# Turning adjacency masks by transposing DMA transfers in a two-layer graph-attention kernel

## The chip, the cores and the metric

The kernel runs on one core of one Trainium2 chip. The metric is the device time of one execution in microseconds (us). A core has several engines that work side by side, each through its own queue in order: TensorE (PE; its weight loads are shown apart as PEld), VectorE (DVE), ScalarE (ACT), GpSimd (POOL) and SyncE (SP), which issues most loads. Sixteen DMA engines move data between HBM and SBUF for all of them. Matrix products land in PSUM[...].

## The reference

Two graph-attention layers over 2708 nodes with 1024 features, each behind a layer norm and with a residual. What matters here is that both layers mask their scores with the adjacency matrix:

```python
# layer 0, x is relu(layernorm(input))
f = x @ Wf + bf
g = x @ Wg + bg
e = jax.nn.relu(f @ g.T)
scores = jnp.where(adj > 0, e, NEG)            # adj: 2708 x 2708 int32
attention = jax.nn.softmax(scores, axis=1)
return attention @ (x @ W + bW)
# layer 1: e = leaky_relu(f1 + f2.T), the same mask, softmax, attention @ h, relu
```

## The kernel before

The nodes are cut into five panels of columns: two of width 586 and three of width 512. A panel is computed with the scores transposed: the 128 partitions of a tile hold the nodes attended to, and its columns the nodes of the panel. The nodes on the partitions come in 11 pairs of tiles, mostly two times 128 rows; one pair has two times 74. Products of blocks use Strassen's scheme in Winograd's form, with seven products (M1 to M7) in place of eight, in fp32.

As the adjacency lies in memory by row, its block must be transposed for this layout. A maker of masks per panel has three steps: `fetch` loads int32 blocks; `convert` makes 0 or -2^100 of them in bf16 on VectorE; `turn` transposes.

```python
    WX, HX = wide, wide // 2                       # wide = 586
    ...
    def mask_maker(p):
        r0, w = panels[p][0][0], width[p]
        k4 = w // P                                # 4; P = 128
        tail = w - k4 * P                          # 74 or 0
        ...
        def convert(q):
            n = rows_of[q]
            a, b = raw.pop(q)
            m = [slot("nm", (P, k4, 2, P), BF)]
            nc.vector.tensor_scalar(m[0][:, :, :, :n], a[:, :, :, :n], 0.0, -BIG, op0=OP.is_le, op1=OP.mult)
            ...
        def turn(q):
            n = rows_of[q]
            m = neg.pop(q)
            mk = slot("mask", (P, 2, WX), BF)
            ps = bank("mk_ps", (P, 2, W), BF)
            for k in range(2):
                for i in range(k4):
                    nc.tensor.transpose(ps[:n, k, i * P:(i + 1) * P], m[0][:, i, k, :n], identb)
            nc.scalar.copy(mk[:n, :, :k4 * P], ps[:n, :, :k4 * P])
            if tail:
                ...                                # the same for the last 74 columns, in another bank
            nc.gpsimd.dma_start(mk_d[p][:n, q], mk[:n, :, :w])   # kept in HBM for layer 1
            mk_sb[p, q] = mk
```

The scores of a panel use it one pair ahead (`behind` puts pieces of other work between the products):

```python
        for q in range(NQ):                        # 11 pairs
            make_until(q + 2)                      # panel 0: norms and transposed rows, hs_d
            if q + 2 < NQ:
                fetch(q + 2)
            ...
            product(q, M1, X, True)                # each loads its operands As from hs_d
            if left_over:
                left_over()                        # M4 of the pair before, finish(q - 1, sb, 1)
            product(q, M6, Z, True)
            product(q, M5, Y, True)
            add(t[:n, hi], Y[:n, :h], m1[:n, hi])
            if q + 1 < NQ:
                convert(q + 1)
            behind(rate, True)
            product(q, M2, X, False)
            ...
            product(q, M7, Z, False)
            ...
            product(q, M3, Y, False)
            add(sa[:n, hi], Y[:n, :h], t[:n, lo])
            finish(q, sa, 0)                       # max(s, 0) + mask on VectorE, running maximum
            if q + 1 < NQ:
                turn(q + 1)
            behind(2 * rate, True)
```

The masks of each panel's first pair are made ahead of its scores by `first_masks`. Layer 1 loads the masks from `mk_d` and does not turn them again. The instructions' order in the queues is chosen by a scheduler from the program's order and its dependences, except where VectorE's order is held.

Of the kernel before, what the change touches and what calls it, by code (L numbers as in the profile page):

```python
# [9 lines left out]
BF = mybir.dt.bfloat16  # L10
I32 = mybir.dt.int32
AF = mybir.ActivationFunctionType
OP = mybir.AluOpType
AX = mybir.AxisListType

BIG = 2.0 ** 100
EPS = 1e-5
ALPHA = 0.2
P = 128
W = 512  # L20
# [36 lines left out]
def kernel(  # L57
# [19 lines left out]
    nc = InOrder(tc)  # L77
# [5 lines left out]
    wide = (N - 3 * W) // 2  # L83
# [6 lines left out]
    tiles = [t for q in panels for t in q]  # L90
# [4 lines left out]
    pairs = []  # L95
# [5 lines left out]
    NQ = len(pairs)  # L101
    pair_of = {t: (q, k) for q, ts in enumerate(pairs) for k, t in enumerate(ts)}
    rows_of = [tiles[a][1] for a, _ in pairs]
    WX, HX = wide, wide // 2

    consts = ctx.enter_context(tc.tile_pool(name="consts", bufs=1))
    slots = ctx.enter_context(tc.tile_pool(name="slots", bufs=54))
# [6 lines left out]
    def slot(name, shape=(P, WX), dt=FP):  # L114
        return slots.tile(list(shape), dt, tag="slot", name=name)

    def stream(name, shape=(P, D), dt=FP):
        return strm.tile(list(shape), dt, tag="strm", name=name)

    def load(o, i):  # L120
        tc.keep_in_program_order(nc.sync.dma_start(o, i))

    def bank(name, shape=(P, W), dt=FP):
        return psum.tile(list(shape), dt, tag="bank", name=name)
# [15 lines left out]

    ident = consts.tile([P, P], FP, name="ident")
    make_identity(nc, ident)
    identb = consts.tile([P, P], BF, name="identb")
    nc.vector.tensor_copy(identb, ident)
    eps = consts.tile([P, 1], FP, name="eps")
    nc.vector.memset(eps, EPS)
    ones = consts.tile([P, 1], FP, name="ones")
# [16 lines left out]
    def one():  # L164
        for it in later[:2]:
            if it[1]:
                it[1]()
                it[1] = None
        us, _, go = later.pop(0)[:3]
        go()  # L170
        return us

    def behind(us, psum_free=False):
        credit[0] = min(credit[0] + us, 2 * us)
        while later and credit[0] > 0 and (psum_free or not later[0][3]) and (not later[0][4] or later[0][4]()):
            credit[0] -= one()
# [41 lines left out]
    def add(o, a, b):  # L218
        nc.vector.tensor_tensor(o, a, b, OP.add)
# [354 lines left out]
    def mask_maker(p):  # L574

        r0, w = panels[p][0][0], width[p]
        k4 = w // P
        tail = w - k4 * P
        raw, neg = {}, {}

        def fetch(q):
            a = stream("adj_i", (P, k4, 2, P), I32)
            b = slot("adj_t", (P, 2, P), I32) if tail else None
            raw[q] = a, b
            (j0, n), (j1, _) = (tiles[t] for t in pairs[q])
            body = adj[r0:r0 + k4 * P].rearrange("(i p) j -> p i j", p=P)
            last = adj[r0 + k4 * P:r0 + w]
            if j1 == j0 + P:
                load(a.rearrange("p i k j -> p i (k j)"), body[:, :, j0:j0 + 2 * P])
                if tail:  # L590
                    load(b[:tail].rearrange("p k j -> p (k j)"), last[:, j0:j0 + 2 * P])
            else:
                for k, j in enumerate((j0, j1)):
                    load(a[:, :, k, :n], body[:, :, j:j + n])
                    if tail:
                        load(b[:tail, k, :n], last[:, j:j + n])

        def convert(q):
            n = rows_of[q]
            a, b = raw.pop(q)  # L600
            m = [slot("nm", (P, k4, 2, P), BF)]
            nc.vector.tensor_scalar(m[0][:, :, :, :n], a[:, :, :, :n], 0.0, -BIG, op0=OP.is_le, op1=OP.mult)
            if tail:
                m.append(slot("nmt", (P, 2, P), BF))
                nc.vector.tensor_scalar(m[1][:tail, :, :n], b[:tail, :, :n], 0.0, -BIG, op0=OP.is_le, op1=OP.mult)
            neg[q] = m

        def turn(q):
            n = rows_of[q]
            m = neg.pop(q)  # L610
            mk = slot("mask", (P, 2, WX), BF)
            ps = bank("mk_ps", (P, 2, W), BF)
            for k in range(2):
                for i in range(k4):
                    nc.tensor.transpose(ps[:n, k, i * P:(i + 1) * P], m[0][:, i, k, :n], identb)  # L615
            nc.scalar.copy(mk[:n, :, :k4 * P], ps[:n, :, :k4 * P])  # L616
            if tail:
                ps = bank("mk_ps", (P, 2, W), BF)
                for k in range(2):
                    nc.tensor.transpose(ps[:n, k, :tail], m[1][:tail, k, :n], identb[:tail, :tail])  # L620
                nc.scalar.copy(mk[:n, :, k4 * P:w], ps[:n, :, :tail])
            nc.gpsimd.dma_start(mk_d[p][:n, q], mk[:n, :, :w])
            mk_sb[p, q] = mk

        return fetch, convert, turn
# [272 lines left out]
    def scores(p, B):  # L898

        w = width[p]  # L900
        h = w // 2
        lo, hi = slice(0, h), slice(h, w)
        fetch, convert, turn = makers[p]
        rb = slot("rb")
        spread(rb, [r_[:n, first[p] + i:first[p] + i + 1] for i, (_, n) in enumerate(panels[p])])
        acc = slot("acc")
        S = [None] * NT
        rate = (0.6, 1.0, 0.65, 0.65, 0.65)[p]
        lefts = {}

        def product(q, m, ps, start):
            n, i = rows_of[q], BY_SCORES.index(m)
            if i % 2 == 0:
                t = stream("As", (P, 2, NH, P))
                lefts[q] = t
                k = min(2, 7 - i)
                if n == P:
                    load(t[:, :k].rearrange("p m c j -> p (m c j)"),
                         hs_d[q][:, i:i + k].rearrange("p m c j -> p (m c j)"))
                else:  # L920
                    load(t[:, :k, :, :n].rearrange("p m c j -> p (m c) j"),
                         hs_d[q][:, i:i + k, :, :n].rearrange("p m c j -> p (m c) j"))
            for c in range(NH):
                nc.tensor.matmul(ps[:n, :h], lefts[q][:, i % 2, c, :n], B[m][c // 2][:, c % 2, :h],  # L924
                                 start=(start and c == 0), stop=(c == NH - 1), skip_group_check=True)

        def finish(q, s, k):

            n, mk = rows_of[q], mk_sb[p, q]
            nc.vector.scalar_tensor_tensor(s[:n, :w], s[:n, :w], 0.0, mk[:n, k, :w], op0=OP.max, op1=OP.add)  # L930
            if q == 0 and k == 0:
                nc.vector.tensor_copy(acc[:, :w], s[:, :w])
            else:
                nc.vector.tensor_tensor(acc[:n, :w], acc[:n, :w], s[:n, :w], OP.max)
            if q in known:
                raise_max(p, q, k, mk[:n, k, :w])

        def last(q, sb, Z, m1):

            n = rows_of[q]  # L940
            product(q, M4, Z, False)
            add(sb[:n, lo], Z[:n, :h], m1[:n, lo])
            finish(q, sb, 1)
            mk_sb.pop((p, q))
            behind(rate, True)

        nc.hold = True
        left_over = None
        for q in range(NQ):
            n = rows_of[q]  # L950
            make_until(q + 2)
            if q + 2 < NQ:
                fetch(q + 2)
            sa, sb = slot("Sa"), slot("Sb")
            S[pairs[q][0]], S[pairs[q][1]] = sa, sb
            X, Y, Z = (bank(f"s{k}") for k in "xyz")
            m1, t = slot("sm1"), slot("st")
            product(q, M1, X, True)
            for s in (lo, hi):
                add(m1[:n, s], X[:n, :h], rb[:n, s])  # L960
            if left_over:
                left_over()
            product(q, M6, Z, True)
            add(t[:n, lo], Z[:n, :h], m1[:n, hi])
            behind(rate, True)
            product(q, M5, Y, True)
            add(t[:n, hi], Y[:n, :h], m1[:n, hi])
            if q + 1 < NQ:
                convert(q + 1)
            behind(rate, True)  # L970
            product(q, M2, X, False)
            add(sa[:n, lo], X[:n, :h], rb[:n, lo])
            behind(rate, True)
            product(q, M7, Z, False)
            add(sb[:n, hi], Z[:n, :h], t[:n, hi])
            behind(rate, True)
            product(q, M3, Y, False)
            add(sa[:n, hi], Y[:n, :h], t[:n, lo])
            finish(q, sa, 0)
            if q + 1 < NQ:  # L980
                turn(q + 1)
            behind(2 * rate, True)
            left_over = lambda q=q, sb=sb, Z=Z, m1=m1: last(q, sb, Z, m1)
        left_over()
        nc.hold = False
        return S, acc
# [279 lines left out]
```

## Time and profile before

| What | Before |
|---|---|
| time, median of 3 | 3197.63 us (3196.51 to 3199.61) |
| span of the profiled execution | 3194.6 us |
| mean granted TensorE clock | 0.992 |
| DMA in the whole span | 649.93 MB, mean 203 GB/s |
| transposes of masks, full blocks | 440, and 44 of the tails |
| copies of masks out of PSUM | 55 of the full blocks, 22 of the tails |
| masks stored to HBM | 55 transfers |

How to read it: the span is the time of one profiled execution. A line of the costliest groups gives line of the program, engine, operation, output and inputs, then count, busy time, mean duration in ns, and the engine's idle time just before with what ended most of it. A duration of a matmul or transpose on TensorE overlaps with its neighbours'. A line of waits gives who waited for whom: us in total, times, longest. A DMA queue's line gives packets, MB, and the time of its packets as a share of 16 engines over the stretch. The helper line L44 stands for all VectorE operations.

### The profile page before, as it was taken

How to read it: one execution, taken by the hardware profiler on the slowest of the kernel's cores; microseconds unless marked ns; L12 is line 12 of the kernel's file. 1: busy time of each engine (PE TensorE's matmuls, PEld its weight loads, DVE VectorE, ACT ScalarE, POOL GpSimd, SP SyncE). 2: the span in 40 equal slices, each digit the busy share in tenths (PEclk: the TensorE clock that was granted, in tenths of full speed). 3: DMA queues.
4: the chain of work that ended last, by engine and by line, in shares of the span. 5: the costliest groups of instructions: out<-in, count | busy, mean ns of one | idle time of the engine just before them, and what ended most of it. 6: DMA issues, size and time to landing. Idle time of an engine off the chain costs nothing.

```text
span 3194.6 us, 35414 instructions
## 1 busy us (share of the span) xinstructions
PE 3124.2 (98%) x12934; PEld 2327.1 (73%) x12934; DVE 1757.6 (55%) x3606; ACT 507.7 (16%) x853; POOL 380.3 (12%) x476
## 2 busy tenths in 40 slices
PE   8999999999999999999999999998999999999998
PEld 5576776667877588876888886865757748778685
DVE  7957676375722686427671358658474371643712
ACT  4412120010200112001020002103031130211200
POOL 3623102110002110011000101020010000000001
PEclk9999999999999999999999999999999999999999
DMA  6958848776446586477755567695655455565655
GB/s 258 330 189 284 284 131 318 216 235 198 165 128 182 173 272 198 147 210 228 246 163 155 163 205 235 200 305 195 206 169 164 142 171 170 186 187 176 195 155 205
DMA packets 284334, 649.93 MB, mean 203 GB/s; under 512 B 51254, under 2 KB 116746, under 8 KB 284160
## 3 DMA queue, kind: packets, MB, share of 16 engines
q1 hardware_dynamic: 243744, 522.94, 51.8%
q0 software_dynamic: 40416, 124.72, 11.5%
q8 instruction: 103, 1.69, 0.2%
q14 instruction: 71, 0.58, 0.1%
HBM read 533.96 MB, written 113.58 MB: 203 GB/s over the span
## 4 chain that ended last, share of the span: by engine, by line
PE 83%; issue 8%; DVE 4%; POOL 2%; DMA 2%; ACT 1%; SPq 0%; POOLq 0%; DVEq 0%; ACTq 0%
PE gz L478 13%; PE gy L478 13%; PE gx L478 12%; PE sz L924 8%; PE sy L924 5%; PE sx L924 5%; PE pz L822 5%; PE gv L478 4%; PE M_ps L413 3%; PE qz L478 3%; PE py L822 3%; PE px L822 3%; PE qy L478 2%; PE qx L478 2%; PE mk_ps L615 1%
## 5 line engine op out<-in xcount | busy, mean ns | idle before, releaser
L924 PE MATMUL sz<-B,As 128*128 128x256 f32 (+3 forms) x1320 | 323.1, 393 | 0.7 <-DVE st L44 0.7
L924 PEld LDWEIGHTS sz<-B,As 128*128 128x128 f32 (+1 forms) x1320 | 245.1, 186 | 58.3 <-DVE st L44 1.7
L924 PE MATMUL sx<-B,As 128*128 128x256 f32 (+3 forms) x880 | 225.0, 399 | 10.2 <-DMA As<-hs_d 9.2
L756 POOL TENSOR_TENSOR gT<-gT,rr 128x2048 f32<-128x2048 f32 (+3 forms) x20 | 68.3, 3432 | 1274.6 <-DVE rr L44 475.7
L924 PE MATMUL sy<-B,As 128*128 128x256 f32 (+3 forms) x880 | 218.8, 391 | 0.0
L478 PE MATMUL gz<-Sa,hc 128*128 128x256 f32 (+3 forms) x880 | 206.6, 393 | 0.0
L478 PE MATMUL gz<-P,hc 128*128 128x256 f32 (+3 forms) x880 | 206.3, 393 | 0.0
L478 PE MATMUL gx<-P,hc 128*128 128x256 f32 (+3 forms) x880 | 202.6, 392 | 0.1
L478 PE MATMUL gy<-T,hc 128*128 128x256 f32 (+3 forms) x880 | 202.5, 391 | 0.0
L924 PEld LDWEIGHTS sx<-B,As 128*128 128x128 f32 (+1 forms) x880 | 161.3, 188 | 46.3 <-issue 11.4
L478 PEld LDWEIGHTS gx<-P,hc 128*128 128x128 f32 (+1 forms) x880 | 167.1, 190 | 35.7 <-issue 2.0
L478 PEld LDWEIGHTS gy<-T,hc 128*128 128x128 f32 (+1 forms) x880 | 166.9, 190 | 34.0
L924 PEld LDWEIGHTS sy<-B,As 128*128 128x128 f32 (+1 forms) x880 | 162.8, 185 | 37.7 <-DVE st L44 0.3
L478 PEld LDWEIGHTS gz<-Sa,hc 128*128 128x128 f32 (+1 forms) x880 | 165.5, 190 | 31.9
L478 PEld LDWEIGHTS gz<-P,hc 128*128 128x128 f32 (+1 forms) x880 | 165.5, 190 | 31.9
L822 PE MATMUL px<-w,gT 128*128 128x512 f32 x320 | 145.5, 607 | 12.5 <-issue 11.1
L822 PE MATMUL py<-w,ps 128*128 128x512 f32 (+1 forms) x352 | 155.3, 592 | 0.0
L822 PE MATMUL pz<-w,ps 128*128 128x512 f32 (+1 forms) x352 | 155.1, 592 | 0.0
L616 ACT COPY mask<-mk_ps 128x1024 bf16<-128x1024 bf16 (+1 forms) x55 | 55.6, 1011 | 555.5 <-PE mk_ps L615 274.2
L822 PEld LDWEIGHTS pz<-w,ps 128*128 128x128 f32 (+1 forms) x352 | 65.4, 186 | 85.6 <-issue 82.0
L822 PEld LDWEIGHTS py<-w,ps 128*128 128x128 f32 (+1 forms) x352 | 65.4, 186 | 85.1 <-issue 82.9
L822 PEld LDWEIGHTS px<-w,gT 128*128 128x128 f32 x320 | 61.6, 195 | 88.7 <-issue 84.1
(261 smaller groups left out, 4790.6 us busy)
## 6 DMA issues: line engine op xcount, KB each, us to landing
hc<-hg_d SPq DMA_DIRECT2D x350, 512.0 KB
As<-hs_d SPq DMA_DIRECT2D x150, 512.0 KB
w<-wt_d SPq DMA_DIRECT2D x96, 512.0 KB
w<-in_L_gnn_W_dram SPq DMA_DIRECT2D x72, 512.0 KB
md<-md_d SPq DMA_DIRECT2D x56, 512.0 KB
adj_i<-in_adj_dram SPq DMA_DIRECT2D x50, 512.0 KB
hg_d<-g POOLq DMA_DIRECT2D x40, 512.0 KB, 5.0
hs_d<-hsT POOLq DMA_DIRECT2D x40, 512.0 KB, 6.1
```

What stands on the lines that cost most here:

```text
L413: nc.tensor.matmul(ps, wfT[a][c // NH][:, c % NH, :], wgT[b][c], start=(c == 0), stop=(c == NC - 1))
L478: nc.tensor.matmul(ps[d], left(m, k, d), right(m, k), start=(start and k == 0), stop=(k == K - 1), skip_group_check=True)
L615: nc.tensor.transpose(ps[:n, k, i * P:(i + 1) * P], m[0][:, i, k, :n], identb)
L616: nc.scalar.copy(mk[:n, :, :k4 * P], ps[:n, :, :k4 * P])
L756: nc.gpsimd.tensor_tensor(of(e, s), of(e, s), by(s, k), OP.mult)
L822: nc.tensor.matmul(ps, left[i][m][:, k, :], w_[k], start=(start and k == 0), stop=(k == NH - 1), skip_group_check=True)
L924: nc.tensor.matmul(ps[:n, :h], lefts[q][:, i % 2, c, :n], B[m][c // 2][:, c % 2, :h], start=(start and c == 0), stop=(c == NH - 1), skip_g ...
```

## The change

`turn` no longer uses TensorE, PSUM and ScalarE's copies. Each block of 128 x 256 bf16 (the two halves of a pair side by side) is transposed by one DMA transfer from SBUF to SBUF, issued from ScalarE's queue; a tail is padded from 74 to 80 rows and takes one more. For this the mask's row is padded from 586 to 592 columns, the padding of the tail's source is cleared on VectorE, short pairs load and convert full blocks of 128 columns, and the identity in bf16 is dropped. `turn` is called straight after `convert`, as its transfers have a latency. It is meant to take the transposes out of TensorE's queue.

```diff
-    WX, HX = wide, wide // 2
+    HX = wide // 2
+    WX = -(-wide // 16) * 16
...
-    identb = consts.tile([P, P], BF, name="identb")
-    nc.vector.tensor_copy(identb, ident)
...
+        tail16 = -(-tail // 16) * 16
...
-                    load(a[:, :, k, :n], body[:, :, j:j + n])
+                    load(a[:, :, k, :], body[:, :, j:j + P])
...
-            nc.vector.tensor_scalar(m[0][:, :, :, :n], a[:, :, :, :n], 0.0, -BIG, op0=OP.is_le, op1=OP.mult)
+            nc.vector.tensor_scalar(m[0], a, 0.0, -BIG, op0=OP.is_le, op1=OP.mult)
             if tail:
                 m.append(slot("nmt", (P, 2, P), BF))
-                nc.vector.tensor_scalar(m[1][:tail, :, :n], b[:tail, :, :n], 0.0, -BIG, op0=OP.is_le, op1=OP.mult)
+                nc.vector.memset(m[1][tail // 32 * 32:tail16], 0.0)
+                nc.vector.tensor_scalar(m[1][:tail], b[:tail], 0.0, -BIG, op0=OP.is_le, op1=OP.mult)
...
             mk = slot("mask", (P, 2, WX), BF)
-            ps = bank("mk_ps", (P, 2, W), BF)
-            for k in range(2):
-                for i in range(k4):
-                    nc.tensor.transpose(ps[:n, k, i * P:(i + 1) * P], m[0][:, i, k, :n], identb)
-            nc.scalar.copy(mk[:n, :, :k4 * P], ps[:n, :, :k4 * P])
+            for i in range(k4):
+                nc.scalar.dma_start_transpose(mk[:, :, i * P:(i + 1) * P], m[0][:, i].rearrange("p k j -> p (k j)"))
             if tail:
-                ps = bank("mk_ps", (P, 2, W), BF)
-                for k in range(2):
-                    nc.tensor.transpose(ps[:n, k, :tail], m[1][:tail, k, :n], identb[:tail, :tail])
-                nc.scalar.copy(mk[:n, :, k4 * P:w], ps[:n, :, :tail])
+                nc.scalar.dma_start_transpose(mk[:, :, k4 * P:k4 * P + tail16],
+                                              m[1][:tail16].rearrange("p k j -> p (k j)"))
...
             if q + 1 < NQ:
                 convert(q + 1)
+                turn(q + 1)
...
             finish(q, sa, 0)
-            if q + 1 < NQ:
-                turn(q + 1)
             behind(2 * rate, True)
```

More of the change, by code (lines that the diff above doesn't have):

```diff
@@ L584, in fetch @@
             raw[q] = a, b
-            (j0, n), (j1, _) = (tiles[t] for t in pairs[q])
+            j0, j1 = (tiles[t][0] for t in pairs[q])
             body = adj[r0:r0 + k4 * P].rearrange("(i p) j -> p i j", p=P)
@@ L593, in fetch @@
                 for k, j in enumerate((j0, j1)):
-                    load(a[:, :, k, :n], body[:, :, j:j + n])
+                    load(a[:, :, k, :], body[:, :, j:j + P])
                     if tail:
-                        load(b[:tail, k, :n], last[:, j:j + n])
+                        load(b[:tail, k, :], last[:, j:j + P])
         def convert(q):
-            n = rows_of[q]
             a, b = raw.pop(q)
             m = [slot("nm", (P, k4, 2, P), BF)]
-            nc.vector.tensor_scalar(m[0][:, :, :, :n], a[:, :, :, :n], 0.0, -BIG, op0=OP.is_le, op1=OP.mult)
+            nc.vector.tensor_scalar(m[0], a, 0.0, -BIG, op0=OP.is_le, op1=OP.mult)
             if tail:
                 m.append(slot("nmt", (P, 2, P), BF))
-                nc.vector.tensor_scalar(m[1][:tail, :, :n], b[:tail, :, :n], 0.0, -BIG, op0=OP.is_le, op1=OP.mult)
+                nc.vector.memset(m[1][tail // 32 * 32:tail16], 0.0)
+                nc.vector.tensor_scalar(m[1][:tail], b[:tail], 0.0, -BIG, op0=OP.is_le, op1=OP.mult)
             neg[q] = m
```

## The prediction

> **What bounds the kernel now.** I read the page's busy table and its chain first. They say which engine to count.
>
> ```profile
> PE 3124.2 (98%) x12934; PEld 2327.1 (73%) x12934; DVE 1757.6 (55%) x3606; ACT 507.7 (16%) x853; POOL 380.3 (12%) x476
> PE 83%; issue 8%; DVE 4%; POOL 2%; DMA 2%; ACT 1%; SPq 0%; POOLq 0%; DVEq 0%; ACTq 0%
> L616 ACT COPY mask<-mk_ps 128x1024 bf16<-128x1024 bf16 (+1 forms) x55 | 55.6, 1011 | 555.5 <-PE mk_ps L615 274.2
> ```
>
> TensorE is busy 98% of the span and carries 83% of the chain. Each microsecond of its queue that goes away should come off the time, unless something makes it wait. ScalarE, which holds the mask copies (the third line: 55 copies, 55.6 us, after 555.5 us of idling), is busy 16%. Its copies cost nothing by themselves.
>
> Next I listed the busy time, granted clock and DMA share of the five stretches in which scores are formed, because masks are turned only there. The columns are: stretch, its length, busy us of PE, PEld, DVE, ACT and POOL, clock, DMA share, GB/s. One line per panel:
>
> ```profile
> 197.00:391.00 194.00, 182.14 (x833) 137.76 (x833) 131.28 (x259) 33.95 (x61) 48.75 (x64) 0.96 0.81 272
> 692.00:823.00 131.00, 131.00 (x593) 98.50 (x591) 72.34 (x134) 9.57 (x16) 4.37 (x8) 1.00 0.67 213
> 1112.00:1239.00 127.00, 125.62 (x632) 106.72 (x631) 92.28 (x190) 12.67 (x15) 12.48 (x17) 1.00 0.81 264
> 1487.00:1614.00 127.00, 125.20 (x632) 106.47 (x631) 88.84 (x176) 10.92 (x12) 9.82 (x13) 1.00 0.79 252
> 1799.00:1926.00 127.00, 127.00 (x647) 108.62 (x646) 74.11 (x145) 10.12 (x10) 8.91 (x12) 1.00 0.65 200
> ```
>
> These stretches total 706 us. PE fills all but the first, and DMA is the next fullest resource: 65 to 81%, against 64% over the whole span (the page's queue shares add to 63.6%). The change takes from the fullest column and gives to the next.
>
> Then I looked at one turn on PE in the timeline, in a narrow panel (columns: start, length, instruction, count):
>
> ```profile
> 1547.36 1.89 PE L924 MATMUL sy<-B,As 128*128 128x256 f32 x8
> 1549.09 0.61 PE L615 MATMUL mk_ps<-identb,nm 128*128 128x128 bf16 x8
> 1549.54 1.95 PE L924 MATMUL sx<-B,As 128*128 128x256 f32 x8
> 1551.32 3.62 PE L924 MATMUL sz<-B,As 128*128 128x256 f32 x16
> ```
>
> The lengths overlap, so the starts must be used. A product takes 1549.09 - 1547.36 = 1.73 us. The eight transposes push the next product back by 0.45 us, and that product takes 1.78 instead of 1.73. A turn therefore costs 0.50 us, far less than the 8 x 219 ns that the mean durations of the group would suggest.
>
> Last, the waits of PE and, for the first score stretch, the DMA queues:
>
> ```profile
> PE sx L924 <- DMA As<-hs_d: 9.2, 3, 4.5
> PE mk_ps L615 <- DVE nm L44: 8.8, 7, 2.5
> ...
> q1 hardware_dynamic: 21715, 32.50, 53.1%
> q0 software_dynamic: 5616, 20.22, 27.5%
> ```
>
> PE loses 8.8 us in seven turns that come before VectorE has converted their mask. It loses 9.2 us to operands arriving late. Small as the latter is, it would grow if the transfers got in each other's way.
>
> [...] No run here has a transposing transfer yet.
>
> [...]
>
> **The change part by part.** *Removed from PE.* Two panels have width 586 (22 turns, with a tail of 74 columns) and three have 512 (33 turns). In a wide panel the timeline has transposes at 261.18, the next product at 261.69, the one after at 263.75. A product there normally takes 1.98 us (257.22 to 259.20), so a turn costs 0.51 + 2.06 - 1.98 = 0.59 us. Sum: 22 x 0.59 + 33 x 0.50 = 13.0 + 16.5 = 29.5 us. The five short pairs are counted as full, a matter of a microsecond. The busy view of the turns' instructions in the five stretches agrees: 29.7 us. The 8.8 us of waits for nm may go as well, but part of that comes back when the next product meets the same VectorE. I count nothing for it in the centre and all of it in the best case: 38 us.
>
> *Removed from ScalarE and PSUM.* 55 copies of 1011 ns, 22 of 288 ns, and one or two banks per pair. All beside other work: 0 on the path.
>
> *Added to VectorE.* 22 clears of 16 partitions of the tail (estimate: under the 282 ns of the tail's conversion, so under 6 us), and five short conversions at 682 instead of 457 ns, 1.1 us. VectorE is 55 to 73% busy in these stretches: 0 to 2 us.
>
> *Added to DMA.* 55 x 4 = 220 transfers of 128 x 256 x 2 B = 65,536 B, and 22 of 80 x 256 x 2 = 40,960 B: 15.3 MB, over 706 us 22 GB/s. How much DMA-engine time that means I estimate from two stretches of the ordinary queue. One has 18,742 packets of 1,508 B at 69.6% of 16 engines over 127 us, or 75 ns each. The other has 1,869 packets of 3,505 B at 35.9% over 57 us, or 175 ns each. Both are 20 B/ns per engine. At that rate one 64 KB transfer is 65,536 / (16 x 20) = 0.2 us of all engines, all together 48 us: 7 points of share. The fullest stretches go from 81 to 88%, still open. But a transpose writes short pieces, and three times the ordinary cost is easily possible: 20 points, which fills the 81% stretches, and late operands then take back some 10 to 20 us. My centre lies between: 10 us given back.
>
> *Moved.* The turn now follows the conversion directly. At 1169.51 VectorE converts a mask that it adds at 1187.04: 0.68 us of work leaves 16.8 us for four transfers, or 4.2 us each if they ran one after the other. Latency alone should be hidden.
>
> Sum: 3197.6 - 29.5 + 10 = 3178 us.
>
> **Rivals.** *Free transfers.* The DMA is not full, ScalarE idles, the slack is 16.8 us. Then 3160 to 3168 us, the whole gain.
>
> *The transposing stream becomes the bound.* [...] 3280 to 3600 us. Nothing in this profile speaks against it[...].
>
> *In-order queues.* ScalarE must wait for the conversion before issuing, and whatever stands behind it waits too. In panels 2 to 4 it does little but mask copies (9.1 of 10.9 us in the fourth stretch), so no harm. In panel 0 it also does norms and copies of turned rows (33.95 us), and GpSimd stores masks and rows on one queue. If those loads come later, PE waits in a stretch that already lacks 12 us: 10 to 30 us, time 3180 to 3200.
>
> **Range and chances.** The best case is set by counting, 3160, and can hardly be beaten: 2% would need 64 us, more than twice the removed queue time. The bad side has no such stop. I give the cheap and middle cases about two chances in three, the stream as bound nearly one in three, with a long tail. Range 3160 to 3340. Faster by over 2%: 0.03; within: 0.66; slower: 0.31.
>
> **What would show it.** PE instructions at the turn's line gone, with products in score stretches starting 1.73 and 1.98 us apart without a gap, confirms the gain. The transposing transfers' queue share says which DMA case holds: 7 points or fewer is cheap, 20 the middle, above 30 the bound. VectorE waiting for a DMA into the mask before its addition, or PE waiting long for As, would make the prediction wrong upwards; both should stay below 20 us. A lasting shortfall confined to the first stretch would point to the in-order queues.

## The result and the profile after

The changed kernel took 3303.43 us (median of 4, 3296.43 to 3305.37), against 3197.07 us before: a ratio of 1.0328, 95% interval 1.0310 to 1.0346. It is slower by 3.3%.

The page of the changed kernel: busy times, chain by engine, and the queue that carries only the transposing transfers (packets, MB, share of 16 engines):

```profile
PE 3132.1 (95%) x12450; PEld 2321.5 (70%) x12450; DVE 1765.7 (53%) x3627; ACT 449.2 (14%) x776; POOL 393.3 (12%) x476
...
q10 hardware_dynamic: 67584, 15.35, 2.8%
...
PE 77%; DMA 7%; issue 7%; DVE 5%; ACTq 2%; ACT 1%; POOL 1%; SPq 0%; POOLq 0%; DVEq 0%
```

The 484 transposes are gone (12934 to 12450 matmuls), yet PE is busy 8 us longer, and DMA has risen from 2 to 7% of the chain. The transfers themselves are small: 15.35 MB, 2.8% of the engines.

The same view by stretches as before, from the first to the last score product of each panel (stretch, length, PE, PEld, DVE, ACT, POOL, clock, DMA share, GB/s):

```profile
204.00:437.00 233.00, 181.07 (x698) 133.07 (x698) 132.03 (x264) 21.58 (x39) 52.31 (x63) 0.88 0.79 231
707.00:878.00 171.00, 156.81 (x619) 116.33 (x619) 99.97 (x205) 3.42 (x6) 14.85 (x21) 0.96 0.81 220
1153.00:1322.00 169.00, 143.57 (x622) 119.94 (x621) 101.59 (x209) 3.63 (x6) 15.68 (x22) 0.92 0.83 228
1553.00:1720.00 167.00, 143.08 (x622) 118.72 (x621) 100.00 (x202) 3.21 (x5) 13.49 (x19) 0.94 0.81 213
1904.00:2040.00 136.00, 133.68 (x618) 114.03 (x618) 79.93 (x156) 0.00 (x0) 15.87 (x19) 1.00 0.89 220
```

PE, nearly full before, now idles 52, 14, 25 and 24 us in panels 0 to 3, and DMA is not full meanwhile. Measured the same way on before's timeline, these stretches were (the prediction's five windows, 706 us, left parts of them out) 186.1, 161.1, 140.1, 143.0 and 138.1 us, 768.3 in all; now they add up to 874.9. The difference of 106.6 us is the whole loss (the two spans differ by 106.3). Panel 4 alone got shorter.

Where nothing is awaited, the turn does cost PE nothing. On PE's timeline, in panel 3 (sx, sy and sz are the PSUM tiles of the score products):

```profile
1650.41 1.89 PE L919 MATMUL sy<-B,As 128*128 128x256 f32 x8
...
1652.13 1.89 PE L919 MATMUL sx<-B,As 128*128 128x256 f32 x8
...
1653.86 1.89 PE L919 MATMUL sz<-B,As 128*128 128x256 f32 x8
```

Starts 1.72 and 1.73 us apart, no gap. The waits say what took the place of the turn. SPq is the queue in which SyncE issues the loads. First before, then after:

```profile
SPq L121 <- PE sz L924: 189.7, 83, 12.2
```

```profile
SPq L122 <- DMA mask<-nm: 363.7, 102, 23.9
...
SPq L122 <- PE sz L919: 55.6, 36, 3.4
...
PE sx L919 <- DMA As<-hs_d: 75.1, 11, 13.6
...
PE sz L919 <- DMA As<-hs_d: 12.7, 3, 9.0
```

The loads wait 363.7 us for masks to land, though the operands As depend on no mask. Before, in the score stretches of panels 1 to 4, they waited mainly for products to free a buffer (189.7 us for sz in all, now 55.6): SyncE ran ahead until buffers ran out. In panel 0 it had no such lead: there it waited most for the rows hg_d and hs_d to be stored (45.6 and 27.4 us). Now it falls behind, and PE waits 87.8 us for operands in place of 9.2. In panel 4, the one that got shorter, SyncE waits only 13.8 us for masks; in the others it is 66 to 97 us.

**Why a load waits for a mask** is seen in the built program and in the trace. In the changed kernel the 1328 transfers that SyncE issues and the 242 that ScalarE issues report their ends on the same eight completion semaphores (DMAHW0 to 7 in the program), given out in turn, 196 or 197 of them on each; GpSimd's 401 report on eight others (DMASW0 to 7). In the program each of the 1570, except the first on a semaphore, stands behind a wait in its own queue until the transfer that had its semaphore before has landed. A piece of SyncE's queue before:

```
As<-hs_d 128x1024 [waits DMAHW7_49,PE_49]
As<-hs_d 128x512  [waits DMAHW0_49,PE_49]
As<-hs_d 128x1024 [waits DMAHW1_49,PE_49]
```

and a turn in ScalarE's queue after:

```
DmaTransposeAnt mask<-nm  128x2x128 [waits DMAHW6_49,DVE_49]
DmaTransposeAnt mask<-nm  128x2x128 [waits DMAHW7_49]
DmaTransposeAnt mask<-nm  128x2x128 [waits DMAHW0_49]
DmaTransposeAnt mask<-nm  128x2x128 [waits DMAHW1_49]
DmaTransposeAnt mask<-nmt 128x2x80  [waits DMAHW3_49,DVE_49]
```

A wide pair takes five of the eight. The next loads that get these semaphores stand still (up to 23.9 us in the waits above) until VectorE has converted the mask (DVE_49), ScalarE has issued the transfer and it has landed, and whatever is behind them in SyncE's queue stands still with them. In the whole program 175 loads follow a mask transfer on its semaphore, 100 of them loads of As; only 9 loads wait for a mask transfer on another semaphore than their own, as they would for a buffer. The reverse holds as well: a turn waits for loads. The chain in panel 3 shows both (start, length, what):

```profile
1657.57 11.19 DMA mask<-nm
...
1669.23 11.18 DMA As<-hs_d
...
1680.48 1.19 ACTq L613
...
1681.71 1.26 ACTq L613
...
1683.01 1.40 ACTq L613
...
1684.45 13.76 DMA mask<-nm
...
1698.33 0.70 DVE Sa L44
```

A mask lands and releases a load; the load lands and releases the next transposes; these land and VectorE can add the mask. Two streams that overlapped have become one after the other.

PE's idleness costs twice. In panel 0 the timeline has

```profile
328.18 2.14 PE L919 MATMUL sy<-B,As 128*128 128x293 f32 x8
343.93 4.28 PE L919 MATMUL sx<-B,As 128*128 128x293 f32 x8 [13.61 <-DMA As<-hs_d]
348.00 5.14 PE L919 MATMUL sz<-B,As 128*128 128x293 f32 x16
```

After 13.61 us of idling, the same eight matmuls take 4.28 us where they took 2.14. The granted clock was 0.50 from 343.93 to 348.21 us, and 1.00 in the 10 us from 350 on. Over the full score stretches PE idles 117.8 us against 19.8 before, and is busy 758.0 us against 749.0. It is busy longer although 32.3 us of transposes are gone, because the same 3080 matmuls of score products take 749.2 us instead of 723.0. 98.0 + 9.0 = 107.0 us, the whole loss up to rounding.

### The profile page after: what moved, and what is told of

The parts are those of the page before. It is cut to its first block, busy times and chain, and to the rows that moved or that the text cites. A ratio compares the mean times of both kernels' runs of the same rounds, so it can differ in the third digit from the quotient of the medians.

```text
span 3300.9 us, 34760 instructions
## 1 busy us (share of the span) xinstructions
PE 3132.1 (95%) x12450; PEld 2321.5 (70%) x12450; DVE 1765.7 (53%) x3627; ACT 449.2 (14%) x776; POOL 393.3 (12%) x476
## 3 DMA queue, kind: packets, MB, share of 16 engines
q1 hardware_dynamic: 243744, 524.11, 52.4%
q10 hardware_dynamic: 67584, 15.35, 2.8%
## 4 chain that ended last, share of the span: by engine, by line
PE 77%; DMA 7%; issue 7%; DVE 5%; ACTq 2%; ACT 1%; POOL 1%; SPq 0%; POOLq 0%; DVEq 0%
PE gz L477 12%; PE gy L477 12%; PE gx L477 11%; PE sz L919 6%; PE pz L817 5%; PE sx L919 4%; PE gv L477 4%; PE px L817 4%; PE sy L919 4%; PE py L817 4%; PE M_ps L412 3%; PE qz L477 3%; DMA mask<-nm 2%; DMA As<-hs_d 2%; PE qy L477 2%
## 5 line engine op out<-in xcount | busy, mean ns | idle before, releaser
L919 PE MATMUL sz<-B,As 128*128 128x256 f32 (+3 forms) x1320 | 336.9, 406 | 29.7 <-DMA As<-hs_d 12.7
L919 PE MATMUL sx<-B,As 128*128 128x256 f32 (+3 forms) x880 | 242.0, 421 | 88.1 <-DMA As<-hs_d 75.1
L919 PEld LDWEIGHTS sz<-B,As 128*128 128x128 f32 (+1 forms) x1320 | 254.9, 194 | 97.9 <-issue 16.4
L919 PEld LDWEIGHTS sx<-B,As 128*128 128x128 f32 (+1 forms) x880 | 173.4, 200 | 136.7 <-DMA As<-hs_d 54.5
L617 POOL DMA_DIRECT2D mk_d<-mask x55 | 43.8, 797 | 703.2 <-DMA mask<-nm 297.0
```

## The experiments

Theory A: the shared completion semaphores couple the loads to the masks. Theory B, the main rival: transposing slows the DMA engines for others. Ratios are to the kernel before on the same chip, with 95% intervals.

**e1 and e2: ordinary copies, on two issuers.** The transposes become plain SBUF-to-SBUF copies of the same bytes, which leaves the masks unturned: the transposition is left out, all else is done. A tail's copy takes its bytes from the first block of nm.

```diff
-                nc.scalar.dma_start_transpose(mk[:, :, i * P:(i + 1) * P], m[0][:, i].rearrange("p k j -> p (k j)"))
+                nc.scalar.dma_start(mk[:, :, i * P:(i + 1) * P], m[0][:, i])    # e1
+                nc.gpsimd.dma_start(mk[:, :, i * P:(i + 1) * P], m[0][:, i])    # e2
```

> The changed kernel with each transposing transfer replaced by an ordinary SBUF-to-SBUF copy of the same bytes on the same ScalarE queue (the masks are left unturned). Theory A (completion semaphores: the loads on SyncE and the transfers on ScalarE take turns on eight completion semaphores, and a load waits for the transfer that had its semaphore before): as slow as the changed kernel, 3270 to 3320 us, SyncE waiting over 250 us for these copies. Theory B (the transposing mode itself slows the DMA engines for the operand loads): 3160 to 3200 us.

> The same ordinary copies, issued from GpSimd, whose transfers have completion semaphores of their own (the masks are left unturned). Theory A: the loads no longer wait for them, 3160 to 3200 us. A variant of A in which the loads wait because the source buffers are held until the copies have landed: still over 3270 us. Theory B says nothing new beyond e1.

e1: 3269.66 us, 1.0241 (1.0225 to 1.0256), at the lower edge of A's range. e2: 3191.41 us, 0.9990 (0.9981 to 0.9999). SyncE's waits in e1, then in e2:

```profile
SPq L122 <- DMA mask<-nm: 300.9, 87, 26.8
```

```profile
SPq L122 <- DMA mask<-nm: 7.2, 2, 6.2
```

With no transposing at all, e1 still has about 70% of the loss ((3269.7 - 3194.2) / 106). Theory B as the main cause falls. From GpSimd, whose transfers report on semaphores of their own (DMASW, 643 transfers in e2's program, none of SyncE's among them), the same bytes leave the loads alone. In e2 the source buffers are held until the copies land just the same, so held buffers are not the cause either. e2 changes the issuing queue together with the semaphores; e3 and e6 to e8 below keep ScalarE's queue. e2 does not reach e4 below; 10.4 of its 23.3 us more of score time are in panel 0 (194.7 against 184.3), where GpSimd also stores rows. That part stays open.

**e3: the turn back at its old place.**

```diff
                 convert(q + 1)
-                turn(q + 1)
...
             finish(q, sa, 0)
+            if q + 1 < NQ:
+                turn(q + 1)
```

> The changed kernel with turn back at its old place after finish, so the transposing transfers stand behind more of the operand loads in the program. Theory A: those loads no longer queue behind the mask, 3190 to 3260 us. Theory B: same bytes at about the same moment, 3290 to 3320 us.

3254.95 us, 1.0193 (1.0178 to 1.0209). The same transfers, the same ScalarE queue, and some 43 us less (1.0328 - 1.0193 of 3195): in the program 83 loads of As, not 100, stand directly behind a mask on a semaphore, and SyncE waits 257.7 us for the full blocks of masks instead of 363.7. Moving the turn forward, meant to give latency more room, made the change worse. The run also speaks against the number of issues from ScalarE, as such, slowing SyncE's.

**e4: no turn at all.** ScalarE copies the converted mask unturned (the tail from the first block); the transposition is left out.

```diff
-            for i in range(k4):
-                nc.scalar.dma_start_transpose(mk[:, :, i * P:(i + 1) * P], ...)
+            nc.scalar.copy(mk[:, :, :k4 * P].rearrange("p k (i j) -> p k i j", j=P), m[0].rearrange("p i k j -> p k i j"))
```

> Neither transposes on TensorE nor transfers: ScalarE copies the converted mask unturned. This measures what the transposes cost TensorE: 29.5 us by my count, so 3160 to 3172 us under both theories.

3167.01 us, 0.9915 (0.9901 to 0.9930): 27.2 us below before, close to the 29.5 counted. ScalarE still copies here, so this is what the transposes cost TensorE.

**e5 and e6: the same bytes in more or fewer transfers.** e5 cuts each 128x256 in two. e6 merges: the converted mask is laid out by half first, so that one transfer holds 128x1024 in a narrow panel, and two hold 128x512 each in a wide one; a narrow panel's mask row is then 512 columns, not 592.

```diff
+            for k in range(2):                                      # e5
+                for i in range(k4):
+                    nc.scalar.dma_start_transpose(mk[:, k, i * P:(i + 1) * P], m[0][:, i, k])
...
-            m = [slot("nm", (P, k4, 2, P), BF)]
+            m = [slot("nm", (P, 2, k4, P), BF)]                     # e6
...
+                nc.scalar.dma_start_transpose(mk.rearrange("p k (i c) -> p (k i) c", c=P),
+                                              m[0].rearrange("p k i j -> p (k i j)"))
```

> The changed kernel with each transfer of 128x256 cut into two of 128x128: the same bytes, twice the transfers (440 and 22 of the tails), at the same place. Theory A (eight completion semaphores shared with the loads, counted per transfer): more loads stand behind a mask, 3330 to 3420 us. Theory B (transposed bytes slow the engines): unchanged, 3290 to 3315 us.

> The changed kernel with the blocks merged: one transfer of 128x1024 per pair in the narrow panels, two of 128x512 and the tail in the wide ones, the same bytes. Theory A: one to three of eight semaphores taken per pair in place of four or five, 3180 to 3250 us. Theory B: unchanged, 3290 to 3315 us.

e5: 3480.00 us, 1.0891 (1.0873 to 1.0910), beyond what I had given A. e6: 3236.64 us, 1.0141 (1.0122 to 1.0160). The bytes are equal; the count of transfers decides. One reason is the number of semaphores taken. A second shows in how long ScalarE's queue takes to issue one (min/median/max in ns). First e5, 128x128 each; then the changed kernel, 128x256; then e6, 128x1024; then e1, an ordinary copy of 128x256:

```profile
L614 ACTq DMA_TRANSPOSE mask<-nm x440: 1109/1252/3066, 164.0 to 2213.5; - x147
```

```profile
L613 ACTq DMA_TRANSPOSE mask<-nm x220: 1182/1265/3492, 164.6 to 2025.9; - x110
```

```profile
L617 ACTq DMA_TRANSPOSE mask<-nm x33: 1247/1249/1682, 1085.9 to 1952.2; - x33
```

```profile
L613 ACTq DMA_DIRECT2D mask<-nm x220: 601/632/1822, 164.3 to 1988.6; - x110
```

Issuing took about 1.25 us at all three sizes, twice an ordinary copy (0.63). By these medians, issued one after the other, four transfers hold a mask back by 5 us, eight by 10, one by 1.25. The runs do not separate the two reasons. This also fits e1's lying some 28 us below the changed kernel (1.0328 - 1.0241 of 3195), an argument that no run isolates; a transposing transfer's packets also took longer than e1's (22 ns against 17, below), which may be part of it.

**e7 and e8: data ready before its turn.** The adjacency is loaded and converted one pair earlier, and the turn stands at the old place. e8 merges as well.

```diff
-            if q + 2 < NQ:
-                fetch(q + 2)
+            if q == 0:
+                fetch(2)
+            if q + 3 < NQ:
+                fetch(q + 3)
...
-            if q + 1 < NQ:
-                convert(q + 1)
-                turn(q + 1)
+            if q == 0:
+                convert(1)
+            if q + 2 < NQ:
+                convert(q + 2)
...
+            if q + 1 < NQ:                # after finish(q, sa, 0)
+                turn(q + 1)
```

> Blocks as in the changed kernel, but the adjacency is loaded and converted one pair earlier and the turn stands at the old place after finish: when its place in the program comes, the data has long been there. Theory A: a transfer is done before a load needs its semaphore, 3160 to 3210 us. Theory B: 3290 to 3315 us.

> Both: merged transfers and conversion one pair earlier. Theory A: 3160 to 3180 us, below the kernel before by most of what e4 gained (27 us). Theory B: 3290 to 3315 us.

e7: 3225.95 us, 1.0102 (1.0087 to 1.0117). e8: 3198.84 us, 1.0015 (1.0008 to 1.0023). Both went A's way, and both missed A's numbers, by 16 and 19 us: the coupling is loosened, not cut. The runs so far, ordered by their loss against before: loads of As directly behind a mask on a semaphore in the built program, SyncE's wait for masks with the tails (us), PE's wait for As (us), loss (us):

| Run | loads of As behind a mask | SyncE's wait for masks | PE's wait for As | loss |
|---|---|---|---|---|
| e5 | 160 | 828.2 | 215.8 | 285.3 |
| after | 100 | 366.4 | 87.8 | 106.4 |
| e1 | 100 | 300.9 | 79.9 | 75.5 |
| e3 | 83 | 272.8 | 76.2 | 60.8 |
| e6 | 31 | 239.1 | 57.3 | 41.9 |
| e7 | 85 | 167.1 | 50.5 | 31.3 |
| e8 | 39 | 107.1 | 39.8 | 4.1 |
| e2 | 0 | 7.2 | 19.3 | -2.8 |
| e4 | 0 | 0 | 12.0 | -27.2 |

The loss follows the two waits without exception. The number of loads behind a mask alone does not set it: e7 has 85, but its masks are ready early, SyncE waits less for them, and it loses less than e6 with 31. By panel, in us:

| Panel | before | after | e4 | e8 |
|---|---|---|---|---|
| 0 | 186.1 | 232.9 | 184.3 | 204.5 |
| 1 | 161.1 | 170.8 | 153.5 | 156.7 |
| 2 | 140.1 | 168.5 | 134.8 | 142.5 |
| 3 | 143.0 | 166.8 | 134.2 | 133.7 |
| 4 | 138.1 | 136.0 | 133.1 | 133.1 |

In panels 3 and 4 the transposes are as good as free: e8 equals e4, which has none. Panel 3 of e8 by the view of stretches:

```profile
1484.00:1618.00 134.00, 133.71 (x621) 114.24 (x620) 99.95 (x203) 3.03 (x5) 12.16 (x20) 1.00 0.98 285
```

DMA share 0.98, and PE, busy 133.71 of 134 us, lacks nothing: with the loads issued early, the busy DMA did no harm here. Of the 30.6 us by which e8's score time exceeds e4's, 20.2 lie in panel 0, where SyncE still waits 55.8 us for masks, 43.3 for the full blocks and 12.5 for the tails, and 7.7 in panel 2. The DMA share is 0.92 in panel 0 and 1.01 in panel 2, so full engines may have a part in this; no run separates the two.

**e9 and e10: by TensorE where SyncE has no lead.** Panel 0 (e9), or 0 and 2 (e10), keep the transposes on TensorE; the others are as in e8.

```diff
+    by_pe = (0,)                          # e10: (0, 2)
...
+            if p in by_pe:
+                ...                       # transposes and copies as before the change
+            elif tail:
                 ...                       # merged transfers
...
+            ahead = 0 if p in by_pe else 1
```

> Panel 0, where SyncE has no room to spare, by TensorE as before; panels 1 to 4 as in e8 (merged transfers, conversion one pair earlier). If the stages add up as measured (before: 186.1 for panel 0; e8: 156.7, 142.5, 133.7, 133.1 for the rest, against 768.3 in all), 752 us of scores and 3177 to 3183 us. If the gain of panels 1 to 4 in e8 was only time shifted out of panel 0: about 3195 us.

> Panels 0 and 2 by TensorE, 1, 3 and 4 as in e8: 186.1 + 156.7 + 140.1 + 133.7 + 133.1 = 749.7 us of scores by the same sum, 3174 to 3182 us; within 3 us of e9.

e9: 3186.14 us, 0.9976 (0.9965 to 0.9986). e10: 3183.98 us, 0.9971 (0.9959 to 0.9983). Both are 8 to 10 us below the kernel before, a third of what e4 allows. In e9 panels 1 to 4 kept what they had in e8 (562.1 us in all, 566.0 in e8), so their gain was not time shifted out of panel 0. Both missed their ranges by 2 to 3 us: panel 0 took 191.6 us in them instead of 186.1. PE waited 14 to 15 us for As there instead of 9.2; why is not explained, for SyncE waits for no mask in that stretch. Score time came to 753.8 us in each, so panel 2 is a tie.

## Why the prediction was wrong

The time lies within the range, but 125 us above the centre and on the other side of the kernel before.

*What bounds, and what a turn costs PE:* right. 29.5 us counted, 27.2 us in e4. That the busy view gave 29.7 us was partly chance: its five windows hold 404 of the 484 transposes, and the full stretches hold 440, with 32.3 us.

*What the transfers cost the DMA engines:* about double the cheap case, well under its triple, which was an estimate of mine that no trace gave. The queue shows 2.8% of the span, about 22 ns for a packet of 227 B (0.028 x 16 x 3300.9 us / 67,584), or 10 B/ns where I had 20 from larger packets; the loads' queue (q1: 524.11 MB in 243,744 packets) had 2150 B a packet. In the stretches it is 7.6 points of share in panel 0 and 10.6 in panel 4, between my cheap case (7) and the middle (20). Not all of it is due to transposing as such. e1's ordinary copies of the same bytes, on the same queue:

```profile
q10 hardware_dynamic: 65824, 15.33, 2.2%
```

That is about 17 ns for a packet of 233 B, or 13 B/ns. At the 20 B/ns estimated from the ordinary queue it would be 12 ns, so about half of the excess was there without transposing.

*The step that failed* is "Latency alone should be hidden", with the 10 us given back that hung on DMA share alone. I asked when VectorE needs the mask, found 16.8 us, and stopped. For VectorE the step nearly held: its additions waited 6.5 us for masks in the whole run, 4.13 of them at 1698.33. But the transfer has other waiters: the loads that come later on its semaphore. SyncE waited 363.7 us for masks, and in place of 10 us given back PE idled 98.0 us more and ran its score products 26.2 us longer. Of the 117.8 us that PE idles before score products, 87.8 are waits for As alone.

*The rivals:* "the transposing stream becomes the bound" named a time near the right one (3280 and up) for a wrong reason; e1 and e8 speak against it. The range reached up to 3340 on its account, so that the time lies in it is luck. No trace before the change showed how fast such a stream is: 3280 to 3600 us was an estimate without a measurement. "In-order queues" had the right idea with the wrong queue: I gave ScalarE's 10 to 30 us in panel 0, and it was SyncE's in four panels, 46.8, 9.7, 28.4 and 23.8 us.

*The signs I named:* the first came true in part: the transposes are gone and starts are 1.73 us apart, but with gaps of up to 13.6 us, so it did not confirm the gain. The queue's share pointed to a cheap to middling case. VectorE's wait for masks stayed below 20 us (6.5). PE's wait for As, 87.8 us against the 20 allowed, told the truth; and the shortfall was not confined to the first stretch. Fewer GB/s (panel 2: 264 before, 228 after) with longer waits for DMA, at a share of 0.83, pointed to a late issue rather than to full engines.

What I could have seen beforehand: the list of semaphores in the built kernel, or in its profile that SyncE's waits in the score stretches of panels 1 to 4 were mostly for products to free a buffer. That told how far it ran ahead, and that this lead was what a new waiter could take.

## What to carry to other kernels

In this kernel a transfer cost what its issuer and its completion semaphore held up, far more than its bytes: SyncE waited 363.7 us for masks whose transfers took 2.8% of the DMA engines. So before moving work to DMA, list what else waits on that queue and those semaphores, and how far the loads run ahead. If a small transfer depends on late data, issue it where it shares nothing with the loads (e2, without a loss where e1 lost 75.5 us, shows this for ordinary copies alone), or make its data ready a stage early (e7), and merge it into as few transfers as possible (e6, e8). Keep it out of stages where the loads have no lead (panel 0 in e9).

## What the runs showed of the hardware that I had not expected

- A transposing transfer held ScalarE's queue about 1.25 us from 128x128 to 128x1024 bf16 (1252, 1265 and 1249 ns), an ordinary copy of 128x256 0.63 us.
- On the DMA engines it ran at about 10 B/ns each in the changed kernel, an ordinary copy of the same bytes at 13; in panel 3 of e8, at a DMA share of 0.98, PE was still busy 133.71 of 134 us.

Not tried: ScalarE's transfers with completion semaphores apart from SyncE's, which by theory A would cut the coupling itself.
